# Adapters' products in float32r parts, and the values' bias joined to the output's, in a two-layer transformer kernel

## The chip, the cores and the metric

The kernel runs on one core of a Trainium2 chip. The core's engines work side by side, each through its own list of instructions in order, and wait for one another by semaphores: TensorE (PE, matrix products), VectorE (DVE), ScalarE (ACT), GpSimd (POOL) and SyncE (SP), which here issues most of the transfers (DMAs). SBUF is the memory on the core, with 128 partitions; a product's result lands in PSUM.

The metric is the device time of one execution in microseconds (us), the median of several runs. Before the change it is 2222.36 us, with runs from 2220.96 to 2223.24.

## The reference

Two layers over x of 8 batches x 512 tokens x 512 channels, all float32. Each has an attention and a feed-forward part, and a layer normalisation follows each part:

```python
x = layernorm(x + attention0(x))     # 16 heads of 32, causal, biases on Q, K, V and O
x = layernorm(x + experts(x))        # 8 experts, the best 2 of each token
x = layernorm(x + attention1(x))     # 8 query heads of 64, 2 key/value heads
x = layernorm(x + ffn(x))            # 1408 hidden, integer weights with scales
```

The change touches the first two. In attention0 the values and the output are

```python
v = x @ WV.T + WV_b
...
return softmax(scores) @ v @ WO.T + WO_b
```

and each expert has low-rank adapters (rank 16) on its two weights:

```python
gup = gup + 2.0 * (x @ gup_lora_A.T) @ gup_lora_B.T
...
out = out + 2.0 * (h @ down_lora_A.T) @ down_lora_B.T
```

## The kernel before

**Attention0** goes through the batches one by one. A batch has four groups g of four heads, and a group has three units u of key blocks: block 0, blocks 1 and 3, block 2. At each step (g, u), TensorE computes the scores (L1356), ScalarE the exponential (L1360), and GpSimd sets the part above the diagonal to zero (L1365, the mask); the product with the values (L1380) is issued one step later, so that TensorE has other work in between. This other work is listed by `plan` for each (g, u): products for values, queries (L1292) and keys (L1300) of the next group, the output projection, turning and routing of the batch before, and merges. A scheduler orders each engine's instructions by its own estimates when the program is built; for the first two products and from the second half of batch 7 to the end of the tail TensorE keeps the order as written. On the chip each engine runs its list in that fixed order. `normalise` sums the exponentials with a product (rs, L1395), then come a copy on ACT (r_inv, L995), a reciprocal on DVE (L1398, 3.34 us), the multiplication into aoT, and a guard's total on GpSimd (g_total, L998).

**Values** are copied out of PSUM by DVE, which adds the bias from `row`, a tile with both bias rows on all partitions (L1287). The output's bias, `row`'s second half, is added to x itself by GpSimd, one instruction of 128x2048 for each batch (L1474).

**The adapters** are merged into the experts' weights in SBUF before use: W + 2AB. One merge (L786) treats one of 6 blocks of 128x512 of two neighbouring experts: two products ps_lora of 16 rows (L781), then for each a copy with factor 2 on ACT (scaled, L792) and an addition to the weight on GpSimd (L794). There are 24 merges: six at (2,0) and six at (3,0) of batches 1 to 6, two after the last scores, and ten around the first tile steps of the experts. The factors lie in the tile `lora`, four experts at a time, at partitions 0, 32, 64 and 96 (16 rows each); its second load is issued in batch 7. Copies `scaled` share two buffers of 128x512 (tag r_inv) with r_inv.

**After attention0** comes a stretch that this text calls the tail: the steps of the first expert tiles (each step: products gate and up ps_gu, turning of h, product down ps_y), and between them the last batch's projection, turning, routing (ps_logits, choose, dispatch with ps_rank, one-hot tables with ps_table) and the merges. Then run the rest of the expert tiles, attention1 and the ffn, whose products take their left operand as a high and a low half in float32r (L1143).

Of the kernel before, what the change touches and what calls it, by code (L numbers as in the profile page):

```python
# [9 lines left out]
F32 = mybir.dt.float32  # L10
# [8 lines left out]
P = 128  # L19
NB = 8  # L20
S = 512
# [22 lines left out]

RARE = 3
LORA = 3 * 512 + 256
EXPERT = UPS * 512

SUM_LOW, SUM_HIGH = 1e-20, 1e20
# [1 line left out]
WIDEST = 2048.0  # L51


V_BQ, V_BK, V_NS, V_SS, V_SG, V_SU = 0, 4, 8, 12, 16, 16 + NHID
N_VEC = 16 + 2 * NHID


def in_order(tc, *engines):
# [46 lines left out]
class Env:  # L105
# [53 lines left out]
    def load_adapters(self, pool):  # L159
        nc, ins = self.nc, self.ins  # L160
        self.lora_sb = pool.tile([P, 2, LORA], F32, name="lora_sb")
        for i in range(2):
            for j in range(4):
                nc.sync.dma_start(out=self.lora_sb[32 * j : 32 * j + R, i, :], in_=ins.lora[i, j])
        self.wr = pool.tile([P, ND, E], F32, name="wr")
        nc.sync.dma_start(out=self.wr, in_=ins.w_router)
        self.ra = pool.tile([R, D], F32, name="ra")
        nc.sync.dma_start(out=self.ra, in_=ins.router_lora_a)
        self.rb = pool.tile([R, E], F32, name="rb")
        nc.sync.dma_start(out=self.rb, in_=ins.router_lora_b)  # L170
# [246 lines left out]
class Router:  # L417
# [4 lines left out]
    def __init__(self, env, keep, pool, small, tmp, dram):  # L422
        nc = env.nc
        self.env, self.nc, self.keep, self.small = env, nc, keep, small
        self.results = dram.tile([(N_FIXED + N_FREE) * P, D], F32, name="results")
        self.rows = dram.tile([NB * S, D], F32, name="rows")
        n = NB * NT
        self.hots = pool.tile([P, TOP_K, n, E], F32, name="r_hots")
        self.weights = keep.tile([P, TOP_K, n], F32, name="r_weights")

        self.ranks = pool.tile([P, TOP_K, n], F32, name="r_ranks")
        self.to_column = pool.tile([P, TOP_K, n], F32, name="r_to_column")
        self.table = pool.tile([P, E * E_TILES], F32, name="r_table")
        nc.gpsimd.memset(self.table, 0.0)
        self.carry = pool.tile([P, E], F32, name="r_carry")
        nc.vector.memset(self.carry, 0.0)


        self.wr = pool.tile([P, ND, 32], F32, name="r_wr")
        nc.vector.memset(self.wr, 0.0)  # L440
        self.gather = pool.tile([P, E], F32, name="r_gather")
        for c in range(ND):
            at = slice(32 * c, 32 * (c + 1))
            nc.vector.tensor_copy(self.gather[at, :], env.ident[at, 32 * c : 32 * c + E])
        scratch = tmp.tile([P, S], F32, tag="r_inv", name="r_scratch", bufs=2)
        self.ra = scratch[:R, :]
        self.rb = tmp.tile([R, E], F32, name="r_rb")

        def numbers(name, shape, pattern, base=0):
            i = tmp.tile([P, *shape], I32, name=f"{name}_i")  # L450
            nc.gpsimd.iota(i, pattern=pattern, base=base, channel_multiplier=0)
            f = pool.tile([P, *shape], F32, name=name)
            nc.vector.tensor_copy(f, i)
            return f


        self.iota = numbers("r_iota", [NT, E], [[0, NT], [1, E]], base=-E)
        self.part = numbers("r_part", [NT, E], [[0, NT], [E_TILES, E]])
        self.tiles = numbers("r_tiles", [N_FREE], [[1, N_FREE]])
        i = tmp.tile([P, 1], I32, name="r_lane_i")  # L460
        nc.gpsimd.iota(i, pattern=[[0, 1]], base=0, channel_multiplier=1)
        self.lane = pool.tile([P, 1], F32, name="r_lane")
        nc.vector.tensor_copy(self.lane, i)
        i = tmp.tile([P, S], F32, tag="r_inv", name="r_columns_i", bufs=2)[:, : E * E_TILES].bitcast(I32)
        nc.gpsimd.iota(i, pattern=[[1, E * E_TILES]], base=0, channel_multiplier=0)
        self.columns = pool.tile([P, E * E_TILES], BF16, name="r_columns")
        nc.vector.tensor_copy(self.columns, i)

        self.ones = pool.tile([P, P], F32, name="r_ones")
        nc.gpsimd.memset(self.ones, 1.0)  # L470
        self.before = pool.tile([P, P], F32, name="r_before")
        nc.gpsimd.affine_select(out=self.before, in_=self.ones, pattern=[[1, P]], compare_op=ALU.is_gt, fill=0.0,
                                base=0, channel_multiplier=-1)
# [277 lines left out]
class Experts:  # L751
# [17 lines left out]
                                   in_=src.rearrange("u p f -> p u f"))  # L769
            at += n * 512  # L770

    def load_lora(self, pool, i):

        self.lora = pool.tile([P, LORA], F32, tag="lora", name=f"lora_{i}")
        for j in range(4):
            self.nc.sync.dma_start(out=self.lora[32 * j : 32 * j + R, :], in_=self.env.ins.lora[i, j])

    def delta(self, ps, e, c):
        j = 32 * (e % 4)
        a, bt = lora_factors(self.lora[j : j + R, :], c)  # L780
        self.nc.tensor.matmul(ps, lhsT=a, rhs=bt, start=True, stop=True)  # L781

    def chunk(self, e, c, n=1):
# [13 lines left out]
class Tiles:  # L797
# [137 lines left out]
        self.hs[0], self.ats[0] = h, self.order[0][1] * EXPERT  # L935
        self.gate_up_to(0, ps("ps_gu"), lambda: None)

    def step(self):
        i = self.next
        self.next += 1  # L940
        if i + 1 < self.n:
            self.gate_up(i + 1, lambda: self.turn_hidden(i))
        else:
            self.turn_hidden(i)
        for n in range(4 if i == 0 else 5, 6):
            if i + n < self.BY_BLOCKS:
                self.fetch(i + n)
        if i + 10 >= self.BY_BLOCKS:
            self.fetch(i + 10)
        self.down(i)  # L950
        if i + 3 < self.BY_BLOCKS:
            self.turn_rows(i + 3)
        if i + 6 >= self.BY_BLOCKS:
            self.pair_back(i + 6)
        if i + 7 >= self.BY_BLOCKS:
            self.blocks(i + 7)
# [257 lines left out]
def attention0(env, guard, keep, routes, experts, dram, p_mm, tiles_ctx):  # L1214
# [8 lines left out]
    with ExitStack() as phase:  # L1223
# [30 lines left out]
        load_xT(0)  # L1254
        load_w(wk, 2, first)
        load_w(wv, 0)
        row = work.tile([P, 2, D], F32, name="row")
        nc.sync.dma_start(out=row, in_=ins.rows.partition_broadcast(P))
        load_w(wq, 1, others)
        load_w(wk, 2, others)  # L1260
        router = Router(env, keep, routes, small, work, dram)
# [3 lines left out]
        for i in range(N_FIXED + N_FREE - RARE, N_FIXED + N_FREE):  # L1265
            nc.sync.dma_start(out=router.results[ts(i, P), :], in_=guard.total)
        load_w(wo, 3)
        experts.load_lora(work, 0)
        for e in range(4):
            experts.load(e)  # L1270

# [7 lines left out]
        def mm(shape, name):  # L1279
            return p_mm.tile(shape, F32, tag="mm", name=name)  # L1280

        def value(b, t):
            ps = mm([P, D], "ps_v")
            for c in range(ND):
                nc.tensor.matmul(ps, lhsT=xts[b][:, c, ts(t, P)], rhs=wv[:, c, :], start=c == 0, stop=c == ND - 1)  # L1285
            vs[t] = own.tile([P, D], F32, tag=f"v{t}", name=f"v{t}")
            nc.vector.tensor_tensor(vs[t], ps, row[:, 0, :], ALU.add)  # L1287

        def query(b, g):
            ps = mm([P, S], "ps_q")  # L1290
# [119 lines left out]
        def plan(b):  # L1410
# [21 lines left out]
                    todo[3, 0].append(merge)  # L1432
            if b == 0:
                todo[1, 0].append(lambda: router.merge_lora(mm([P, ND, E], "ps_wr")))
            if b > 1:
                todo[0, 2].append(lambda: dispatch(b - 2))
                todo[1, 1].append(lambda: enter(one_hot(b - 2, range(NT))))
# [12 lines left out]
                tiles.fetch(i, room[:, i, :])  # L1450

        def begin():
            pair = work.tile([P, 2, D], F32, tag="row", name="first_turned")
            one = work.tile([P, S], F32, tag="logits", name="first_turned")
            tiles.begin([pair[:, 0, :], pair[:, 1, :], one], work.tile([P, 256], F32, name="first_h"),
                        lambda name: mm([P, S], name))

        def soon():
# [8 lines left out]
        for b in range(NB):  # L1467
            todo = plan(b)
            for g in range(ND):
                if g == 2:  # L1470
                    if b + 1 < NB:
                        load_xT(b + 1)

                    nc.gpsimd.tensor_tensor(xs[b], xs[b], row[:, 1:2, :].to_broadcast([P, NT, D]), ALU.add)  # L1474
                if g == 3 and b + 1 < NB:
                    load_x(b + 1)
                if b == NB - 1 and g == 1:
                    experts.load_lora(work, 1)
                    experts.load(4)
                if b == NB - 1 and g == 2:  # L1480
                    order.enter_context(in_order(tc))
# [32 lines left out]
            merge()  # L1514
        for c in range(ND):
            turn(b, c)
        tiles.step()
        score(b)
        merge()
# [3 lines left out]
        dispatch(b)  # L1523
        for places in ((0, 1), (2, 3)):
            rows = one_hot(b, places)
            tiles.step()
            merge()
        enter(rows)
        tiles.of_fixed = router.fixed(routes)
        while merges:  # L1530
            tiles.step()
            merge()
        order.close()
    return router, tiles, router.tables(routes, p_mm.tile([P, E], F32, tag="mm", name="ps_count"), guard.routed[:, 1:2])
# [569 lines left out]
def _layout(a):  # L2104
# [26 lines left out]
    def columns(n):  # L2131
        return a[n].transpose(0, 2, 1).reshape(2, 4, R, -1)

    lora = np.concatenate([rows("L0_ffn_gup_lora_A"), columns("L0_ffn_gup_lora_B"), columns("L0_ffn_down_lora_B"),
                           rows("L0_ffn_down_lora_A")], axis=3)
    return {
        "x": x,
        "xT": x.transpose(0, 2, 1),
        "w_attn0": np.concatenate([(by_group if n in "QK" else units)(a[f"L0_attn_W{n}_w"].T) for n in "VQKO"]),
        "vecs": np.concatenate(  # L2140
            [cols(a[n]) for n in ("L0_attn_WQ_b", "L0_attn_WK_b", "L1_attn_norm_scale", "L1_attn_split_scale",
                                  "L1_ffn_s_gate", "L1_ffn_s_up")], axis=1),
        "rows": np.stack([a["L0_attn_WV_b"], a["L0_attn_WO_b"]]),
        "w_router": a["L0_ffn_gate_weight"].T.reshape(ND, P, E).transpose(1, 0, 2),
        "router_lora_a": a["L0_ffn_gate_lora_A"],
# [26 lines left out]
```

## Time and profile before

One execution was profiled. It took 2228.55 us, of which the core's span from first to last instruction is 2226.8; it ran 6.2 us above the median of the three timed runs.

| stage (us of the span) | length | PE busy | DVE | ACT | POOL | granted clock |
|---|---|---|---|---|---|---|
| batch 0 of attention0 (0 to 90) | 90 | 84.52 | 36.88 | 27.65 | 27.89 | 1.00 |
| batches 1 to 7 (90 to 720) | 630 | 621.75 | 397.00 | 188.75 | 191.16 | 1.00 |
| end of attention0, tail (720 to 830) | 110 | 105.03 | 61.83 | 31.87 | 38.26 | 0.91 |
| expert tiles (830 to 1185) | 355 | 353.24 | 111.74 | 81.77 | 82.31 | 1.00 |
| attention1 (1185 to 1700) | 515 | 514.32 | 402.37 | 167.48 | 127.12 | 1.00 |
| ffn (1700 to 2226.8) | 526.8 | 512.98 | 263.88 | 134.45 | 20.88 | 0.99 |

The table is from the view by windows: the busy time of each engine in a stretch, and the mean clock that the throttle granted TensorE (1.00 is full speed). A busy TensorE is one with products in flight; it need not be at its peak. In a timeline's lines stand the start in us, the time up to the end of a group of like instructions, engine, line of the code, operation, output and inputs with their shapes, and in brackets the idle time of the engine ahead of it and the engine whose work ended it. A row of the waits names an engine's instruction, whom it waited for, the total in us, how often, and the longest.

In the page's list of groups, the 96 records of the adapters' products (L781, two for each product) have 36.7 us busy, the 48 copies L792 27.1 (599 ns each), the 48 additions L794 62.0 (1313 ns), and the 8 additions of the bias to x L1474 37.2 (4650 ns).

### The profile page before, as it was taken

The numbers are of one execution on the slowest core, as the hardware profiler recorded it, in microseconds if no ns is written. First come the engines' busy times: TensorE is split into PE (matmuls) and PEld (weight loads), VectorE is DVE, ScalarE is ACT, GpSimd is POOL, SyncE is SP. The second block draws the span as 40 slices with busy tenths as digits, with TensorE's granted clock in tenths as the row PEclk, the third lists the DMA queues.
The fourth block names the chain that finished last, engine by engine and source line by source line (L and its number), as shares of the span: only waits on it lengthen the run. The fifth ranks groups of instructions, "written<-read, shape, count | busy, mean of one in ns | idle before, by whom it ended". The sixth has DMA issues, their size and how long they took to land. (4 is left out here: it accounts for less than half of the span.)

```text
span 2226.8 us, 23678 instructions
## 1 busy us (share of the span) xinstructions
PE 2191.9 (98%) x9006; PEld 1116.6 (50%) x9006; DVE 1273.7 (57%) x2032; ACT 632.0 (28%) x917; POOL 487.6 (22%) x489
## 2 busy tenths in 40 slices
PE   9999999999999999999999999999999999999997
PEld 3344444444444444444443333333343778888876
DVE  3556666666666633323316887798757655555443
ACT  2332323323233232122124333223332222222222
POOL 2322423234132333122105222222211000000000
PEclk9999999999999899999999999999999999999999
DMA  8010101101022216888735212312110321111000
GB/s 297 20 57 1 57 10 48 58 1 58 5 71 94 85 57 181 227 218 214 191 114 193 80 57 86 95 55 77 45 32 13 109 78 57 57 57 57 20 20 21
DMA packets 146428, 182.20 MB, mean 82 GB/s; under 512 B 60530, under 2 KB 89202, under 8 KB 144514
## 3 DMA queue, kind: packets, MB, share of 16 engines
q1 hardware_dynamic: 135024, 144.91, 21.0%
q0 software_dynamic: 10560, 34.61, 5.5%
q8 instruction: 74, 1.21, 0.2%
q10 hardware_dynamic: 722, 1.07, 0.1%
q14 instruction: 48, 0.39, 0.1%
HBM read 117.38 MB, written 63.18 MB: 81 GB/s over the span
## 5 line engine op out<-in xcount | busy, mean ns | idle before, releaser
L903 PE MATMUL ps_gu<-experts,xrT 128*128 128x512 f32 (+1 forms) x520 | 248.8, 601 | 0.0
L1360 ACT ACTIVATE p<-sc 128x2048 f32<-128x2048 f32 (+1 forms) x96 | 152.8, 1592 | 190.0 <-PE sc L1356 183.1
L1148 DVE SCALAR_TENSOR_TENSOR hT<-ps_u,vec,sg 128x512 f32<-128x512 f32 x88 | 65.6, 745 | 195.2 <-PE ps_u L1143 195.2
L1365 POOL TENSOR_SCALAR_AFFINE_SELECT p<-p 128x512 f32<-128x512 f32 x128 | 91.6, 729 | 385.2 <-ACT p L1360 378.5
L1159 PE MATMUL ps_f<-ffn_w,h_half 128*128 128x512 f32 x672 | 170.2, 394 | 0.6 <-issue 0.4
L998 POOL TENSOR_TENSOR g_total<-g_total,r_inv 128x512 f32<-128x512 f32 x64 | 89.7, 1401 | 358.3 <-DVE r_inv L1735 283.0
L1705 ACT ACTIVATE p<-sc 128x1024 f32<-128x1024 f32 x128 | 124.0, 1021 | 105.9 <-PE sc L1702 100.8
L1735 DVE RECIPROCAL r_inv<-r_inv 128x512 f32<-128x512 f32 x32 | 107.1, 3346 | 78.8 <-ACT r_inv L995 78.8
L1388 DVE TENSOR_TENSOR p<-p 128x1536 f32<-128x1536 f32 (+2 forms) x96 | 129.4, 1348 | 39.2 <-POOL p L1365 22.2
L905 DVE TENSOR_TENSOR h<-ps_gu,h 128x256 f32<-128x256 f32 x67 | 28.4, 424 | 212.8 <-ACT h L904 212.8
L903 PEld LDWEIGHTS ps_gu<-experts,xrT 128*128 128x128 f32 x520 | 96.2, 197 | 89.7 <-issue 89.5
L1159 PEld LDWEIGHTS ps_f<-ffn_w,h_half 128*128 128x128 f32 x672 | 124.4, 188 | 33.0 <-DVE h_half L1154 5.6
L1143 PE MATMUL ps_g<-x_high,ffn_w 128*128 128x512 f32 x352 | 138.9, 395 | 0.8 <-DVE x L1676 0.8
L1143 PE MATMUL ps_g<-x_low,ffn_w 128*128 128x512 f32 x352 | 139.1, 395 | 0.0
L1143 PE MATMUL ps_u<-x_low,ffn_w 128*128 128x512 f32 x352 | 138.8, 394 | 0.0
L1143 PE MATMUL ps_u<-x_high,ffn_w 128*128 128x512 f32 x352 | 138.7, 394 | 0.0
L919 PE MATMUL ps_y<-experts,hT 128*128 128x512 f32 (+1 forms) x272 | 127.9, 593 | 0.5 <-ACT hT L913 0.5
L1702 PE MATMUL sc<-qT,kT 64*128 64x512 f32 x512 | 127.3, 615 | 1.0 <-ACT qT L1609 0.7
L1292 PE MATMUL ps_q<-experts 128*128 128x512 f32 x256 | 121.1, 615 | 4.4 <-DMA experts<-in_xT 4.4
L1724 PE MATMUL av<-p,v 128*64 128x512 f32 x512 | 123.8, 605 | 0.0
L1285 PE MATMUL ps_v<-experts 128*128 128x512 f32 x256 | 118.0, 609 | 3.3 <-DVE v L1287 3.3
L1670 PE MATMUL ps_o<-attn_out,aoT 128*128 128x512 f32 x256 | 117.9, 605 | 0.8 <-ACT r_inv L995 0.8
(262 smaller groups left out, 3438.5 us busy)
## 6 DMA issues: line engine op xcount, KB each, us to landing
results<-y SPq DMA_DIRECT2D x68, 256.0 KB, 2.3
turned<-turned SPq DMA_DIRECT2D x56, 256.0 KB, 4.1
pair<-xrT SPq DMA_DIRECT2D x25, 512.0 KB, 3.4
xrT<-pair SPq DMA_DIRECT2D x100, 128.0 KB, 4.5
x<-in_x SPq DMA_DIRECT2D x8, 1024.0 KB, 7.5
experts<-in_gate_up SPq DMA_DIRECT2D x8, 1024.0 KB, 10.8
rows<-x SPq DMA_DIRECT2D x32, 256.0 KB, 2.0
x<-rows SPq DMA_DIRECT2D x8, 1024.0 KB, 15.5
```

The costliest lines, as they stand in the source:

```text
L903: nc.tensor.matmul(ps, lhsT=xT[:, c, :], rhs=self.weights(i, c), start=c == 0, stop=c == ND - 1)
L919: self.nc.tensor.matmul(ps, lhsT=hT[:, c, :], rhs=self.weights(i, ND + c), start=c == 0, stop=c == self.NI - 1)
L1143: nc.tensor.matmul(ps, lhsT=w[:, ts(dc, P)], rhs=x[:, dc, :], start=(dc, i) == (0, 0), stop=(dc, i) == (ND - 1, 1))
L1159: self.nc.tensor.matmul(os[t], lhsT=h[:, ts(t, P)], rhs=self.weights(2 * NHID + c), start=(c, i) == (0, 0), stop=(c, i) == (NHID - 1, 1))
L1285: nc.tensor.matmul(ps, lhsT=xts[b][:, c, ts(t, P)], rhs=wv[:, c, :], start=c == 0, stop=c == ND - 1)
L1292: nc.tensor.matmul(ps, lhsT=wq[:, g, ts(c, P)], rhs=xts[b][:, c, :], start=c == 0, stop=c == ND - 1)
L1360: nc.scalar.activation(p, sc[:, :, :width], AF.Exp, scale=scale)
L1388: nc.vector.tensor_tensor(total[:, :, P * kt :], total[:, :, P * kt :], p[:, :, at : at + w], ALU.add)
L1670: nc.tensor.matmul(ps, lhsT=state[b]["aoT"][:, c, ts(t, P)], rhs=w_out[:, c, :], start=c == 0, stop=c == ND - 1)
L1702: nc.tensor.matmul(sc[:, j, :], lhsT=st["kT"][hs, ts(kt, P)], rhs=st["qT"][g][hs, :], start=True, stop=True)
L1705: nc.scalar.activation(p, sc, AF.Exp, scale=scale)
L1724: nc.tensor.matmul(st["av"][HD * j : HD * (j + 1), :], lhsT=st["v"][:, kt, HD * j : HD * (j + 1)], rhs=p[:, j, :], start=kt == 0, stop=kt ...
```

## The change

**Adapters.** The factors are no longer multiplied as float32. Each is split into a high part (its value rounded to float32r) and a low part (the rest), and the four products of parts are computed as one product: the 16 rows of a factor are repeated four times in the input, so that an expert has 64 rows and a pair of experts all 128 partitions. In rows 0 to 15 of an expert stand high parts of both factors, in the others high and low, low and high, low and low. `masks` makes two columns of signs and of zeros and ones from the bits of the partition's number; with them `split_part` makes the parts: ACT copies the raw values with the sign as factor and rounds (l_high), GpSimd multiplies the raw values by 0 or 1 and adds l_high, so that a row has either the high part or raw minus high. A pair's 1792 columns are fetched and split in four pieces (512, 512, 512, 256). There is one buffer for the raw piece; the next piece's fetch is issued after the split of the one before. l_high shares the two r_inv buffers.

The pieces are split in batch 0 at (2,1), (2,2), (3,1), (3,2), in batches 4 and 7 at (0,0), (0,2), (1,0), (1,2), and the last pair's in the tail, two around each of two tile steps, where merges stood. The last six merges now go two a tile step, one in the middle of it and one behind it, over three steps.

**Bias of the values.** Rows of softmax sum to one, so the bias of v passes through to WV_b @ WO.T. `join_bias`, once in batch 0 at (1,2), computes this with four products and adds it to `row`, which now has only the output's half. The copies of the values are plain ones, by DVE for the even and ACT for the odd blocks (`evacuate`). The addition of `row` to x[0] now comes after join_bias.

The two rooms that the first tiles took from `row` are now one from it and one from the raw piece's buffer. The path for rare inputs is adapted (it does not run here), and the input layouts follow. The diff, cut:

```diff
...
-V_BQ, V_BK, V_NS, V_SS, V_SG, V_SU = 0, 4, 8, 12, 16, 16 + NHID
-N_VEC = 16 + 2 * NHID
+V_BQ, V_BK, V_NS, V_SS, V_SG, V_SU, V_BV = 0, 4, 8, 12, 16, 16 + NHID, 16 + 2 * NHID
+N_VEC = V_BV + 4
+LORA_PARTS = 4
...
-    def load_lora(self, pool, i):
-        self.lora = pool.tile([P, LORA], F32, tag="lora", name=f"lora_{i}")
-        for j in range(4):
-            self.nc.sync.dma_start(out=self.lora[32 * j : 32 * j + R, :], in_=self.env.ins.lora[i, j])
+    def masks(self, pool, lane):
+        nc = self.nc
+        bits = pool.tile([P, 2], I32, name="l_bits")
+        self.low = pool.tile([P, 2], F32, name="l_low")
+        self.sign = pool.tile([P, 2], F32, name="l_sign")
+        for i, bit in enumerate((2 * R, R)):
+            nc.vector.tensor_scalar(bits[:, i : i + 1], lane, bit, None, ALU.bitwise_and)
+        nc.vector.tensor_copy(self.low, bits)
+        nc.vector.tensor_scalar(self.low, self.low, 1.0, None, ALU.min)
+        nc.vector.tensor_scalar(self.sign, self.low, -2.0, 1.0, ALU.mult, ALU.add)
+        self.parts = [(q, c) for q in range(E // 2) for c in range(LORA_PARTS)]
+
+    def fetch_part(self, pool):
+        if self.parts:
+            q, c = self.parts[0]
+            at, n = 512 * c, min(512, LORA - 512 * c)
+            self.raw = pool.tile([P, 512], F32, tag="raw", name="l_raw")
+            self.nc.sync.dma_start(out=self.raw[:, :n], in_=self.env.ins.lora[q, :, at : at + n])
+
+    def split_part(self, pool):
+        nc = self.nc
+        q, c = self.parts.pop(0)
+        if c == 0:
+            self.lora = pool.tile([P, LORA], F32R, tag="lora", name=f"lora_{q}")
+        at, n = 512 * c, min(512, LORA - 512 * c)
+        i = int(c in (1, 2))
+        high = pool.tile([P, 512], F32R, tag="r_inv", name="l_high", bufs=2)[:, :n]
+        nc.scalar.activation(high, self.raw[:, :n], AF.Copy, scale=self.sign[:, i : i + 1])
+        raw = self.raw[:, :n]
+        nc.gpsimd.tensor_scalar(raw, raw, self.low[:, i : i + 1], None, ALU.mult)
+        nc.gpsimd.tensor_tensor(self.lora[:, at : at + n], raw, high.bitcast(F32), ALU.add)
+        if (q, c) != (E // 2 - 2, LORA_PARTS - 1):
+            self.fetch_part(pool)
 
     def delta(self, ps, e, c):
-        j = 32 * (e % 4)
-        a, bt = lora_factors(self.lora[j : j + R, :], c)
+        j = P // 2 * (e % 2)
+        a, bt = lora_factors(self.lora[j : j + P // 2, :], c)
         self.nc.tensor.matmul(ps, lhsT=a, rhs=bt, start=True, stop=True)
...
-    def step(self):
+    def step(self, amid=lambda: None):
...
             self.fetch(i + 10)
+        amid()
         self.down(i)
...
-        row = work.tile([P, 2, D], F32, name="row")
-        nc.sync.dma_start(out=row, in_=ins.rows.partition_broadcast(P))
+        row = work.tile([P, D], F32, name="row")
+        nc.sync.dma_start(out=row, in_=ins.rows[1].partition_broadcast(P))
...
-        experts.load_lora(work, 0)
+        experts.masks(work, router.lane_i)
+        experts.fetch_part(work)
         for e in range(4):
             experts.load(e)
...
-            nc.vector.tensor_tensor(vs[t], ps, row[:, 0, :], ALU.add)
+            env.evacuate(t, vs[t], ps)
+
+        def join_bias():
+            bv = work.tile([P, ND, P], F32, tag="r_inv", name="bv", bufs=2)
+            nc.vector.tensor_copy(bv, vec[:, V_BV : V_BV + ND, None].to_broadcast([P, ND, P]))
+            ps = mm([P, D], "ps_bias")
+            for c in range(ND):
+                nc.tensor.matmul(ps, lhsT=bv[:, c, :], rhs=wo[:, c, :], start=c == 0, stop=c == ND - 1)
+            nc.vector.tensor_tensor(row, ps, row, ALU.add)
...
+            if b == 0:
+                todo[1, 2].append(join_bias)
+            early = (0, 0), (0, 2), (1, 0), (1, 2)
+            slots = {0: ((2, 1), (2, 2), (3, 1), (3, 2)), 4: early, 7: early}
+            for slot in slots.get(b, ()):
+                todo[slot].append(lambda: experts.split_part(work))
...
-                    nc.gpsimd.tensor_tensor(xs[b], xs[b], row[:, 1:2, :].to_broadcast([P, NT, D]), ALU.add)
+                    nc.gpsimd.tensor_tensor(xs[b], xs[b], row[:, None, :].to_broadcast([P, NT, D]), ALU.add)
...
                 if b == NB - 1 and g == 1:
-                    experts.load_lora(work, 1)
                     experts.load(4)
...
         for c in range(ND):
             turn(b, c)
+        experts.fetch_part(work)
         tiles.step()
...
         for places in ((0, 1), (2, 3)):
             rows = one_hot(b, places)
+            experts.split_part(work)
             tiles.step()
-            merge()
+            experts.split_part(work)
         enter(rows)
         tiles.of_fixed = router.fixed(routes)
         while merges:
-            tiles.step()
+            tiles.step(merge)
             merge()
...
+    lora = np.repeat(lora.reshape(E // 2, 2, 1, R, LORA), 4, axis=2).reshape(E // 2, P, LORA)
```

## The prediction

> **What bounds the kernel now.** First the busy shares.
>
> ```profile
> PE 2191.9 (98%) x9006; PEld 1116.6 (50%) x9006; DVE 1273.7 (57%) x2032; ACT 632.0 (28%) x917; POOL 487.6 (22%) x489
> ```
>
> TensorE sets the time nearly everywhere: a change gains what it takes off PE and loses what it makes PE wait. PE's waits come next.
>
> ```profile
> PE sc L1356 <- ACT p L1360: 5.2, 7, 1.8
> ...
> PE av L1380 <- POOL p L1365: 0.3, 1, 0.3
> ```
>
> PE waits seven times for an exponential (5.2 us in all; one wait is 1.77, so the other six are 0.58 each) and once, in batch 0, for GpSimd's mask. The timeline shows where a merge stands.
>
> ```profile
> 232.46 1.03 PE L781 MATMUL ps_lora<-lora 16*128 16x512 f32 x4
> 233.41 0.64 PE L1380 MATMUL av<-p,v 128*32 128x256 f32 x8
> 234.63 1.15 PE L1356 MATMUL sc<-q,k 32*128 32x384 f32 x16 [0.58 <-ACT p L1360]
> ```
>
> ```profile
> 811.77 1.13 PE L781 MATMUL ps_lora<-lora 16*128 16x512 f32 x4
> 812.83 1.98 PE L903 MATMUL ps_gu<-experts,xrT 128*128 128x512 f32 x4
> ```
>
> A merge holds PE for 233.41 − 232.46 = 0.95 us in attention, where a wait follows at once, and for 812.83 − 811.77 = 1.06 in the tail, where none does. What one pass at float32r costs, layer 1's FFN shows: starts 0.24 apart.
>
> ```profile
> 1822.73 0.39 PE L1143 MATMUL ps_g<-x_high,ffn_w 128*128 128x512 f32 x1
> 1822.97 0.40 PE L1143 MATMUL ps_g<-x_low,ffn_w 128*128 128x512 f32 x1
> ```
>
> Last, batch 0, where four of the new splits and the bias go.
>
> ```profile
> 54.67 1.59 POOL L998 TENSOR_TENSOR g_total<-g_total,r_inv 128x512 f32<-128x512 f32 x1 [2.03 <-DVE r_inv L1398]
> 56.23 5.51 POOL L1474 TENSOR_TENSOR x<-x,row 128x2048 f32<-128x2048 f32 x1
> ...
> 61.68 1.81 POOL L1365 TENSOR_SCALAR_AFFINE_SELECT p<-p 128x512 f32<-128x512 f32 x3
> 62.37 1.07 PE L1380 MATMUL av<-p,v 128*32 128x512 f32 x8 [0.35 <-POOL p L1365]
> ...
> 68.61 0.69 ACT L1302 ACTIVATE k<-ps_k,vec 128x512 f32<-128x512 f32 x1 [2.58 <-PE ps_k L1300]
> 69.50 1.14 PE L1356 MATMUL sc<-q,k 32*128 32x512 f32 x8
> ```
>
> One addition of 5.51 us on GpSimd holds up the mask behind it, and PE runs out of cover: GpSimd is 22% busy over the span but the limit here.
>
> **The gain: 24 merges.** A merge has two products of two passes each; starts of passes lie 0.43 apart, and the two products run side by side on different rows, 0.9 to 1.06 a merge. In float32r a product is one pass; if the pair still runs side by side, 0.24 to 0.4 is left, a gain of 0.63. Where it arrives differs:
> - Six merges at (2,0) of batches 1 to 6: the exponential sets the pace behind them, so the wait grows from 0.58 to 1.2 and nothing is gained.
> - Six at (3,0): the second product sits among the scores (253.94), and scores and merge take 253.93 to 255.86 = 1.93 against 235.71 − 234.63 = 1.08 for scores alone. Gain (1.93 − 1.08) − 0.2 = 0.65 each, 3.9.
> - Two after the last scores hold PE 737.63 to 742.64, 5.0 us, as a chain: product, ACT's copy (0.60 each), next product. Four copies and the first product stay, about 3.1: gain 1.9.
> - Ten in the expert tiles: 10 × 0.63 = 6.3.
> - The 0.74 that PE waits for ACT's copy ahead of the table (820.70) goes, since no merge stands there now: 0.7.
> Sum −12.8. The bounds: nothing where a longer wait swallows all (the six at (3,0) and the ten: −2.6), or 24 × 0.7 + 2.6 = −19.4 where none does.
>
> The Trainium skill, "TensorEngine Tiling (Array Packing)", in Key Properties, says that a change of tiling mode makes the array drain; a 64-row product amid 32-row scores would be one. The 16-row products among the scores showed no gap (253.94, 253.95). By the page, at an estimate of 0.3 a time from the length of a 32-row score pass (8 of them in 1.14 us, two of those), six such places would take 1.8 off the gain, and the sum would be +11.6; no run here shows it.
>
> **Values.** Their evacuation is still one pass from PSUM (0.69 on DVE before; now two on DVE, two on ACT at 0.60 to 0.69). PE's four waits for them (3.3 us in all) come from DVE's chain for the routing, and v0 remains on DVE behind it: 0, bounds −3.3 to +1.
>
> **The bias, on PE's path.** join_bias adds four float32 products 128x512 in batch 0's (1,2): 8 records × 0.43 = 3.44. They wait for a copy on DVE (0.68) that stands behind a reciprocal (51.25 to 54.6), while PE is ready at 54.4: 0.9. Sum +4.4; bounds +3.4 and +5.5.
>
> **Batch 0's splits.** Each of 16 splits is: ACT copy 0.6, GpSimd multiplication by a value per partition (nearest row L721: 1.56 alone, 2.54 beside gathers; I take 1.65), GpSimd addition (L722 1.26 to 1.59, L794 mean 1.31; 1.35), then the next fetch, of 256 KB (rows of that size land in 2.0 to 2.3, the 112 KB of the old adapter loads in 3.0 to 4.3; 3.1). There is one buffer, so the next ACT copy stands in ACT's order until its fetch lands, and all later work of ACT with it.
> - First stall. The first copy needs the buffer of g_total's operand, free at 56.3: copy 57.0, multiplication 58.7, addition 60.1. In the order built for GpSimd, both row additions of x follow (the one of 19.69, which now needs the joined row, and the one of 56.23), at 4.5 to 5.5 each: 69.3; then the mask, 69.95. PE wants it at 62.0 + 4.4 = 66.4: +3.5. Before, 5.5 us of addition were just covered (0.35); that cover is spent.
> - Second stall. ACT's order has r_inv, copy 1, p(2,2), copy 2, k(3). From r_inv at 72.2: 0.6 + 1.65 + 1.35 + 3.1 + 0.6, then k's 0.69, gives 80.2, or 80.9 with the mask and g_total of GpSimd between; PE is ready at 69.5 + 4.4 + 3.5 = 77.4: +3.5.
> - After each wait PE runs slower, below: +3.2.
> Sum +10.2; bounds 0 (fetch and splits in half the time) and +14.
>
> **The clock.** A wait of 1.77 us at 722.9 is followed by
>
> ```profile
> 720.00:724.00 4.00, 2.23 (x26) 0.86 (x22) 3.33 (x19) 2.00 (x2) 0.66 (x1) 0.91 0.67 258
> 724.00:728.00 4.00, 4.00 (x28) 1.96 (x24) 3.41 (x20) 1.88 (x1) 1.22 (x2) 0.50 0.02 4
> 728.00:732.00 4.00, 3.41 (x24) 1.38 (x16) 3.99 (x10) 2.17 (x5) 0.39 (x1) 0.74 0.00 0
> ```
>
> the eighth column being the granted clock: 0.50 for 3.4 to 6 us, so 1.7 to 3 us of work lost. One of 1.71 at 277.3 does the same; the waits of 0.58 do not. The six waits of 1.2 us lie between: 0 to 6 × 1.7 = +10 by that; I take one loss, +2. The skill's "TensorE: Matmul & The Clock Gate", Part 1: The HAM clock gate, wants a whole idle window of some 3.4 us; the row at 724 contradicts it with 1.77. By the page this term would be 0 and the sum +7.8.
>
> **Batches 4 and 7.** A split's copy stands before k(1) of ACT, at 0.3 to 1.2 each: +1. SP's order gets three small fetches between the loads of experts 4 and 5 (660.3 and later), whose first use is in the tail, tens of us on: 0, and at most a fetch's 3 us each if that slack were gone. In batch 0 one fetch replaces four of 112 KB ahead of the experts' loads: 0. The masks are five instructions on single columns at the start, the third room of begin only a new place: 0.
>
> **The tail.** Four splits fall around three tile steps, each fetch starting after the addition. ACT's copies stand ahead of h and hT: h 0.7 late; the next hT waits for a chain of 2.5 us of older additions and three times (GpSimd 3.0, fetch 2.8, copy 0.6), 21.2 after the ranks, where PE is there at 19.0, so 2.6 to 3.4 with hT's own copy; then the last six merges, two a step, need 2 × 1.3 on GpSimd each, and the gathers for later tiles (0.95) queue behind: 1.5. Sum +5; bounds 0 and +9.
>
> **Sum.** −12.8 + 4.4 + 10.2 + 2 + 1 + 5 = +9.8. The profiled execution took 2228.55 us (span 2226.8), so 2238.4 in its terms. It lay 6.2 above the median of the runs, 2222.4, which I carry over: 2232.2.
>
> **Rivals.**
> - *Everything hides* (faster). GpSimd and ACT have slack, the fetches land in 2 us, nothing waits in batch 0 or the tail. For it: 22% and 28% busy. Against it: the 0.35 at 62.37, where one addition already overran. Then −12.8 + 4.4 = −8.4: 2214.0. It decides if a split takes under 3 us from copy to landed fetch.
> - *Half of it hides* (no change). Only batch 0's first stall and its clock appear, 3.5 + 1.5, and 3.5 in the tail: −12.8 + 4.4 + 8.5 = +0.1, 2222.5.
> - *The clock falls at every (2,0)* (slower still). Six waits of 1.2 us each bring half speed: +8 more, and the tail costs 9: 2232.2 + 8 + 4 = 2244.
> - *The pair doesn't run side by side*. 64-row products in turn cost 0.46 a merge, 16 × 0.23 = 3.7 less gain: 2236; within the forecast's range.
>
> **How the numbers follow.** Forecast with its fourth rival 0.48 (own range 2226 to 2239), everything hides 0.22, half hides 0.18, clock at every (2,0) 0.12. The measurement can tell 0.2%, 4.4 us. Forecast and last case lie above 2226.8, half hides between the bounds, everything hides below 2217.9: slower 0.60, same 0.18, faster 0.22. The range leaves out half of "everything hides" below 2213 and most of the last case above 2243.
>
> **What would show it.** Right: in batch 0 an av waiting for GpSimd's p for some 3.5 us and a sc for ACT's k for another 3.5, clock 0.50 behind each; four ps_bias products of 3.4 us; ps_lora in two records that take 0.25 to 0.4 together; (2,0) waits of 1.2 without half clock; an hT or ps_y in the tail waiting for ACT 2 to 3 us. Wrong: no wait over 1 us in 55 to 85 (first rival), clock 0.5 after each (2,0) (third), or ps_lora records 0.43 apart (no gain at all: 2245). What would upset it most: a fetch much faster than 3 us.

## The result, and the profile after

The change makes the kernel slower, by 0.3%: 2229.61 us (median of 12 runs, 2227.26 to 2233.28) against 2223.34 (12 runs, 2220.96 to 2226.88); ratio 1.0026, 95% interval 1.0018 to 1.0034. The forecast was 2232, slower.

Busy shares after, from the page's first part:

```profile
PE 2177.5 (98%) x8966; PEld 1111.3 (50%) x8966; DVE 1270.7 (57%) x2023; ACT 650.1 (29%) x949; POOL 528.5 (24%) x521
```

TensorE is busy for 14.4 us less than in the first profile of before (2191.9), and 6.7 less than in a second one (2184.2, with the experiments); most of what these two differ by is clock, 23.9 and 10.2 us at half speed ahead of the last instructions. Yet the time rose: more of it is spent waiting. The waits of TensorE after (waiter, whom it waited for, total us, times, longest):

```profile
PE av L1426 <- POOL p L1411: 4.1, 1, 4.1
...
PE ps_y L954 <- ACT hT L948: 3.3, 2, 2.8
PE sc L1402 <- ACT k L1348: 3.0, 2, 2.2
```

The three hardly stood in the profile of before (0.3, 0.5 and 0.8). The waits for the exponential, at the head of that view, grew from 5.2 to 7.8: six of 0.58 are 1.0 now. Of the three, the wait for the mask and most of that for k are in batch 0. TensorE there, from the timeline:

```profile
70.53 1.07 PE L1426 MATMUL av<-p,v 128*32 128x512 f32 x8 [4.07 <-POOL p L1411]
71.42 1.86 PE L1441 MATMUL rs<-p,ones 128*32 128x512 f32 x8
...
81.94 1.14 PE L1402 MATMUL sc<-q,k 32*128 32x512 f32 x8 [2.21 <-ACT k L1348]
```

and the two engines that it waits for, GpSimd and then ScalarE:

```profile
60.90 8.99 POOL L1525 TENSOR_TENSOR x<-x,row 128x2048 f32<-128x2048 f32 x2
69.83 1.83 POOL L1411 TENSOR_SCALAR_AFFINE_SELECT p<-p 128x512 f32<-128x512 f32 x3
```

```profile
80.60 0.72 ACT L805 ACTIVATE l_high<-l_raw,l_sign 128x512 fp32r<-128x512 f32 x1 [4.98 <-DMA l_raw<-in_lora]
81.22 0.67 ACT L1348 ACTIVATE k<-ps_k,vec 128x512 f32<-128x512 f32 x1
```

The mask that TensorE wants at 66.5 stands behind one split (57.11 to 60.9) and both additions of `row` (8.99 together), and comes at 69.83. The copy of k stands behind a copy of raw factors whose fetch has not landed. The rs behind the first wait take 1.86 instead of 1.04; the windows give the reason (the eighth column is the granted clock):

```profile
66.00:70.00 4.00, 0.46 (x2) 0.00 (x0) 0.75 (x1) 0.54 (x1) 4.00 (x2) 1.00 0.00 0
70.00:74.00 4.00, 3.47 (x24) 0.93 (x24) 1.76 (x1) 0.60 (x3) 1.65 (x3) 0.69 0.00 0
```

After TensorE's 4.07 us of nothing, the clock is down once, for 3.4 us at half speed (0.69 here and 0.89 in the next four: the missing 0.31 and 0.11 of 4 us each make 1.7 us, the half of 3.4); from 78 on, around the second wait, it is 1.00. Such a stretch of 3.4 us is called a half-clock window below.

Where the merges stand, TensorE after, at (2,0):

```profile
244.54 0.49 PE L816 MATMUL ps_lora<-lora 64*128 64x512 f32 x2
244.97 0.64 PE L1426 MATMUL av<-p,v 128*32 128x256 f32 x8
```

A pair side by side holds TensorE 0.43, in the tail as well (848.07 to 848.50), where it was 0.95 to 1.06. At (3,0), before (batch 2) and after (batch 1):

```profile
252.31 1.12 PE L781 MATMUL ps_lora<-lora 16*128 16x512 f32 x2
253.36 0.64 PE L1380 MATMUL av<-p,v 128*32 128x256 f32 x8
253.93 0.58 PE L1356 MATMUL sc<-q,k 32*128 32x384 f32 x1
253.94 0.69 PE L781 MATMUL ps_lora<-lora 16*128 16x512 f32 x1
253.95 0.92 PE L1356 MATMUL sc<-q,k 32*128 32x384 f32 x5
...
255.86 1.13 PE L1292 MATMUL ps_q<-experts 128*128 128x512 f32 x2
```

```profile
171.25 0.49 PE L816 MATMUL ps_lora<-lora 64*128 64x512 f32 x1
171.68 0.64 PE L1426 MATMUL av<-p,v 128*32 128x256 f32 x8
172.32 0.91 PE L1402 MATMUL sc<-q,k 32*128 32x384 f32 x2
173.16 0.50 PE L816 MATMUL ps_lora<-lora 64*128 64x512 f32 x1
173.59 1.14 PE L1402 MATMUL sc<-q,k 32*128 32x384 f32 x14
174.66 0.70 PE L1338 MATMUL ps_q<-experts 128*128 128x512 f32 x1
```

Here a merge's two products stand apart, the first ahead of the products with the values, the second among the scores. The first held TensorE 1.05 (two passes) and holds 0.43. The second ran beside the scores before (253.93 to 253.95); now one score's two passes run alone, then the product alone, then the other scores, and the stretch from the first score to ps_q takes 2.34 instead of 1.93.

The kernel of before was profiled a second time with the experiments (span 2219.4, time 2221.15, nearer the median than the first). Like products of the two programs were laid side by side, and the difference of their starts followed through the span:

| stretch | start after − start before, at its end | step | forecast |
|---|---|---|---|
| first transfers | 1.1 | +1.1 | 0 |
| join_bias | 5.3 | +4.2 | +4.4 |
| two waits in batch 0 and the clock | 13.3 | +8.0 | +10.2 |
| batches 1 to 7, merges at (2,0) and (3,0) | 14.7 | +1.4 | −3.9 + 1 + 2 |
| merges and tail, up to the tables | 6.0 | −8.7 | −8.9, late merges included |
| last pair's splits, late merges | 11.1 | +5.1 | +5 |
| attention1 and ffn | 7.9 | −3.2 | 0 |

The two profiled executions differ by 8.1 (2227.5 − 2219.4), the medians by 6.3. The 1.1 of the first transfers belongs to the execution: the run below with the first splits in batch 1 starts as after does and lacks it. The +1.4 of batches 1 to 7 is −0.8 at (3,0), +1.3 in waits for values (3.3 against 2.0) and +0.9 in the clock at the end of batch 7; the last two differ from one execution to the next.

### The profile page after: what moved, and what is told of

The parts are those of the page before. It is cut to its first block, busy times and chain, and to the rows that moved or that the text cites. A ratio compares the mean times of both kernels' runs of the same rounds, so it can differ in the third digit from the quotient of the medians.

```text
span 2227.5 us, 23696 instructions
## 1 busy us (share of the span) xinstructions
PE 2177.5 (98%) x8966; PEld 1111.3 (50%) x8966; DVE 1270.7 (57%) x2023; ACT 650.1 (29%) x949; POOL 528.5 (24%) x521
## 5 line engine op out<-in xcount | busy, mean ns | idle before, releaser
L1340 DVE TENSOR_SCALAR q<-ps_q,vec 128x512 f32<-128x512 f32 x32 | 24.0, 751 | 180.4 <-PE ps_q L1338 180.4
```

## The experiments

All times are medians but for the last; each ratio is to runs of the kernel before on the same chip. "Fastest" is "both remedies, bias as before".

| kernel | us | ratio, 95% interval |
|---|---|---|
| after | 2229.61 | 1.0026 (1.0018 to 1.0034) |
| before, again | 2223.24 | 0.9998 (0.9989 to 1.0007) |
| bias alone | 2228.90 | 1.0022 (1.0011 to 1.0032) |
| after, first splits in batch 1 | 2223.46 | 0.9999 (0.9988 to 1.0009) |
| after, last pair fetched at once | 2226.28 | 1.0014 (1.0003 to 1.0025) |
| both remedies | 2219.33 | 0.9976 (0.9967 to 0.9985) |
| both remedies, bias as before | 2214.10 | 0.9955 (0.9942 to 0.9967) |
| splits in batch 0, bias as before | 2220.43 | 0.9984 (0.9974 to 0.9993) |
| before, vec wider | 2222.11 | 0.9991 (0.9983 to 1.0000) |
| fastest, buffers at 64 | 2217.26 | 0.9979 (0.9967 to 0.9991) |
| fastest, buffers at 96 | 2216.57 | 0.9966 (0.9955 to 0.9978) |
| both remedies, products over 128 rows | 2218.49, one run | |

**Before, unchanged.** No edit.

> The kernel of before, unchanged, profiled a second time. Its median should be 2223 again. The two profiled executions differ in layer 1's FFN: starts of products there are 0.2327 us apart on average before and 0.2312 after, some 3.4 us over the FFN, though no part of the change touches it. If that belongs to the one execution that was profiled, this profile shows another average; if it belongs to the program (its place in memory), it shows 0.2327 again and the change would gain 3.4 us there that nobody meant.

Two products of the FFN in this profile, and the same two in the profile after:

```profile
1735.01 0.39 PE L1159 MATMUL ps_f<-ffn_w,h_half 128*128 128x512 f32 x1
...
2185.76 0.39 PE L1143 MATMUL ps_u<-x_high,ffn_w 128*128 128x512 f32 x1
```

```profile
1745.93 0.62 PE L1195 MATMUL ps_f<-ffn_w,h_half 128*128 128x512 f32 x2
...
2193.77 0.39 PE L1179 MATMUL ps_u<-x_high,ffn_w 128*128 128x512 f32 x1
```

450.75 us lie between them before and 447.84 after, over 1936 starts: 0.2328 us each and 0.2313 (the expectations count 0.0001 less). The first profile of before has 0.2328 as well. So the FFN's gain of some 3 us belongs to the program and not to the execution, though the change does not touch the FFN.

**Before, with the buffers moved.**

```diff
-N_VEC = 16 + 2 * NHID
+N_VEC = 16 + 2 * NHID + 4
```

> Before, with nothing changed but vec four columns wider (38 to 42), which moves every later buffer by 16 bytes. If the FFN's shorter spacing (0.2312 instead of 0.2327 on average) comes from where its buffers lie, the spacing is 0.2312 here too and the time 2223.4 - 3.3 = 2220. Rival, it comes from another part of the bias change: 0.2327 and 2223.4.

In the built program the later buffers lie 32 bytes further on, not 16, since rooms are rounded up. Spacing 0.2313, as after; by the same two products the FFN gains 2.9 us. The time is 2222.11; against the runs of before on its chip (2224.64) that is −2.5, with an interval that reaches 1.0000, so it is the spacing that shows it. The two later runs below, with the buffers 64 and 96 bytes from where before has them, show 0.2337 and 0.2332. So the FFN's gain comes from where the buffers lie, and not by a rule of 64 bytes.

**The bias alone.**

```diff
-            nc.vector.tensor_tensor(vs[t], ps, row[:, 0, :], ALU.add)
+            env.evacuate(t, vs[t], ps)
...
+            if b == 0:
+                todo[1, 2].append(join_bias)
```

> Before, with only the bias joined to the output's and the plain copies of the values; adapters as before. Theory: the four products cost 4.2, and since the addition of the row to x[0] now follows them on GpSimd, both additions (4.5 each) stand ahead of the masks of batch 0's third group: row ready at 59.6, masks at 69.3 where PE is there at 66.5, a wait of 2.5 to 3 where it was 0.35, perhaps with one half-clock window (1.7): 2223.3 + 4.2 + 2.5 + 0.9 = 2231. Rival 1, only the products count: 2227.5. Rival 2, the plain copies of the values give back what the products cost: 2223.

Measured 2228.90, and 2231 less the FFN's 3 is 2228. TensorE waits 2.88 for the mask without a single split in the program. GpSimd of this kernel:

```profile
59.61 8.98 POOL L1484 TENSOR_TENSOR x<-x,row 128x2048 f32<-128x2048 f32 x2 [3.46 <-DVE row L1296]
68.55 1.80 POOL L1374 TENSOR_SCALAR_AFFINE_SELECT p<-p 128x512 f32<-128x512 f32 x3
```

Both additions start when the joined row is there (59.61) and hold up the masks for 9 us. Before, the first of them ran at 19.69, long before anything needed GpSimd. The bias part alone loses 5.4 us against before on its chip, nearly as much as the whole change. In the trace, by the starts of like products, its products cost 4.2 and the wait behind the addition that had to move 2.5, and the FFN gives 3.2 back. Another 4.8 come in batches 2 to 6 of this execution, with longer waits for values (5.3 in all, against 2.0 in the second profile of before) and a half-clock window behind one of them; whether the plain copies have a part in that is not shown.

**First pair's splits in batch 1.**

```diff
-            slots = {0: ((2, 1), (2, 2), (3, 1), (3, 2)), 4: early, 7: early}
+            slots = {1: early, 4: early, 7: early}
```

> After, with the first pair's four splits in batch 1 at the early steps that batches 4 and 7 use, none in batch 0. Theory: the wait of sc for k (2.21) goes, of the wait of av for GpSimd's mask (4.07) only the 1.2 that the split stood ahead of the additions goes, since the two additions make the rest, and batch 1 has no new wait over 1 us: 2229.6 - 2.2 - 1.2 - 0.8 = 2225.5. Rival 1, the splits make both waits: 2229.6 - 6.3 - 1.7 = 2221.6. Rival 2, the splits cost the same wherever they stand: 2229.6.

Measured 2223.46, 6 us less than after. The wait for k is gone, the wait for the mask (68.08) still 2.89, as the theory had it. In the trace, the difference to after is −1.3 (first transfers) at the start, −5.1 at the end of batch 0 and −6.2 in batch 5; at the head of batch 2 there is one new wait for values, of 0.97. That the time came out 2 below the theory's 2225.5 is of the size of that first difference and of the waits for values, which differ between executions.

**Last pair's factors fetched at once.**

```diff
+    def fetch_last(self, pool):
+        room = pool.tile([P, ND, 512], F32, tag="aoT", name="l_last")
+        self.nc.sync.dma_start(out=room.rearrange("p c s -> p (c s)")[:, :LORA], in_=self.env.ins.lora[E // 2 - 1])
+        self.last = [room[:, c, :] for c in range(LORA_PARTS)]
...
         experts.load(7)
+        experts.fetch_last(work)
...
-        experts.fetch_part(work)
```

> After, with the last pair's raw factors fetched in one transfer, ahead of the tail's tile steps, into the buffer that aoT leaves free, so that no split in the tail waits for a fetch; the work of ACT and GpSimd on them is the same. Theory: the chain of fetches set the tail's waits; ps_y's wait for hT (2.76), ps_hT's for h (0.59) and the half-clock window behind them (1.7) go: 2229.6 - 5 = 2224.6. Rival: GpSimd's chain of splits, additions and gathers sets the tail, and the wait only moves to the merges behind: 2228 to 2229.6.

Measured 2226.28, between the two. After, TensorE and ScalarE in the tail:

```profile
825.66 0.50 PE L816 MATMUL ps_lora<-lora 64*128 64x512 f32 x2
828.92 3.48 PE L954 MATMUL ps_y<-experts,hT 128*128 128x512 f32 x4 [2.76 <-ACT hT L948]
```

```profile
828.10 0.51 ACT L805 ACTIVATE l_high<-l_raw,l_sign 128x256 fp32r<-128x256 f32 x1 [5.04 <-DMA l_raw<-in_lora]
828.52 0.35 ACT L948 COPY hT<-ps_hT 128x256 f32<-128x256 f32 x1
```

and with the single fetch:

```profile
816.48 0.44 PE L953 MATMUL ps_hT<-ident,h 128*128 128x128 f32 x2 [1.47 <-DVE h L947]
```

The wait of 2.76 and the half-clock window behind it are gone, and a wait of 1.47 stands in their place (by the starts of like products the tail gains 4.7, by the medians 3.3): now ScalarE's copies wait for GpSimd's 2.9 us a split (the last until 815.14), and h (815.55) stands behind them. Both theories were half right.

**Both remedies, and with the bias as before.** The second is the first with the value's bias on DVE, both halves of `row`, and the raw pieces in the buffer of the logits, since there is no room for one of their own beside a whole `row`; a pair's first piece is then fetched in the last step of the batch before its splits.

```diff
-            env.evacuate(t, vs[t], ps)
+            nc.vector.tensor_tensor(vs[t], ps, row[:, 0, :], ALU.add)
...
-                todo[1, 2].append(join_bias)
...
-            self.raw = pool.tile([P, 512], F32, tag="raw", name="l_raw")
+            self.raw = pool.tile([P, 512], F32, tag="logits", name="l_raw")
```

> After, with both remedies for the splits (first pair's in batch 1, last pair's factors fetched at once into aoT's buffer) and the joined bias kept. If the two remedies add up: 2229.6 - 6.1 - 3.3 = 2220.2. Against the kernel without the joined bias it tells what the bias costs in batch 0: theory 4.2 of products and 2.5 of wait of av for GpSimd's mask, so 6.7 and perhaps half a clock window more than that kernel.

> The adapters' parts alone, with their splits where they cost least: the values' bias is added by DVE as before and row keeps both halves (no join_bias), the first pair's splits stand in batch 1, the last pair's raw factors are fetched at once into aoT's buffer, and the other raw pieces take the buffer of the logits (there is no room for one of their own). Theory: from the 2223.5 of the splits in batch 1, less 3.3 (the tail, as measured) and less the bias's products and the addition behind them (4.2 + 2.5): 2213.5, faster than before by 10. Rival: in the bias kernels layer 1's FFN gains 3.3 us that come with the bias; without it they are lost and the time is 2217. If the FFN's gain comes from vec's four more columns, which this kernel keeps, it stays.

2219.33 and 2214.10: the remedies add up, and the second kernel is the fastest of all, 0.45% below before. Some 3 of these 10.5 us are the FFN's, from the four columns of vec, which this kernel keeps and does not use. At the end of batch 0 the one with the joined bias is 7.1 us later by the trace, beside the 0.6 of the first transfers (4.2 products, 3.0 the wait), but only 5.2 by the median. In the two profiled executions, 2.4 more are lost at the end of batch 7, where the clock falls in the one with the joined bias alone, and 3.9 come back at 740, where the fastest kernel shows a wait that the other lacks:

```profile
PE ps_lora L823 <- DVE first_h L947: 3.4, 1, 3.4
```

The reason is in the clock (eighth column) and in DVE's timeline. This kernel's:

```profile
724.00:728.00 4.00, 3.53 (x33) 1.52 (x32) 3.88 (x19) 2.53 (x5) 1.50 (x3) 1.00 0.03 6
```

```profile
734.99 1.37 DVE L581 TENSOR_SCALAR one_hot<-r_columns,r_to_column 128x256 bf16<-128x256 bf16 x1
```

and those of its twin with buffers at 64, with the same order of instructions:

```profile
724.00:728.00 4.00, 4.00 (x24) 0.91 (x16) 3.93 (x17) 0.84 (x3) 1.22 (x2) 0.50 0.01 2
```

```profile
734.44 0.28 DVE L581 TENSOR_SCALAR one_hot<-r_columns,r_to_column 128x256 bf16<-128x256 bf16 x1
```

In the first the clock stays up behind the wait of 1.76, and TensorE's merge starts at 733.74. GpSimd adds two merged blocks at 735.01 to 737.51, the two instructions of DVE beside them take 1.3 instead of 0.3, and first_h, behind them on DVE, comes at 738.42. In the second the clock falls, the merge starts at 735.51 and the additions at 736.78, behind first_h (735.80). Of the thirteen profiles two have the clock up there, this one and the next run's, and these two alone have the wait of 3.4: what the kernel is spared by the clock it loses again here.

**Splits in batch 0, bias as before.** The kernel just shown, with the slots of the change and the first fetch at (0,0) of batch 0.

> Bias added by DVE as before, with the first pair's splits left in batch 0, as the change has them (raw pieces in the logits' buffer, last pair's factors fetched at once). In GpSimd's order both additions to x now stand ahead of the first split. Theory: against the kernel with the joined bias and the same tail (2226.3) the products (4.2) and the wait of av for the mask (4.07) go, the wait of sc for k (2.2) behind the fetch stays: about 2217.5. Rival: the split alone holds up the masks as much as the two additions did, and the wait of av stays at 3 to 4: 2222.

Measured 2220.43, again between: the products are gone, TensorE waits 1.50 for a mask (58.07) and 2.33 for k (73.97). Here the first split alone holds up the mask, and its multiplication takes 3.10 (52.98). So the wait for k belongs to the fetch and the order of ScalarE, whatever the bias does. Of after's 4.07 the split makes 1.2, by the run with the splits in batch 1. This profile too has the wait of 3.4 for first_h.

**Products over 128 rows.** The kernel with both remedies, each product over all rows. It sums over both experts of the pair, so its merged weights are not those of the reference; it serves to price the product.

```diff
-        a, bt = lora_factors(self.lora[j : j + P // 2, :], c)
+        a, bt = lora_factors(self.lora, c)
```

> The kernel before this one in the list, but with each adapters' product taken over all 128 rows (it sums over both experts of the pair, so the merged weights are others), so that no product uses part of the array's rows. After, a pair of 64-row products holds TensorE 0.43 in the tail and in attention, and a single one at (3,0) also 0.43, where a float32r pass of 128 rows in the FFN takes 0.23. If the change between 64 and 128 rows costs the 0.2 (and 0.1 ahead of it), two 128-row products take 0.46 together in the tail and a single one at (3,0) 0.23. If a lone float32r product behind float32 ones costs 0.43 whatever its rows, the pair takes 0.86.

One run, 2218.49. Products at (2,0):

```profile
145.82 0.74 PE L823 MATMUL ps_lora<-lora 128*128 128x512 f32 x2
146.49 0.64 PE L1433 MATMUL av<-p,v 128*32 128x256 f32 x8
```

Two take 0.67 (0.34 and 0.33). One alone at (3,0) takes 0.42 (165.57 to 165.99), as one of 64 rows does, so a second one adds 0.25. The second expectation is right for a lone product and wrong for the pair: the 0.2 extra comes once for the float32r products that stand together among the attention's, and not from 64 rows. The scores around the second product at (3,0) take 2.34 here too (166.64 to 168.98). In the tail, from the start of the turning ahead of the merge to the gate product behind it, two products of 128 rows in turn take 0.90 (823.53 to 824.43), and after's pair of 64 rows 0.96 (847.54 to 848.50). Side by side or in turn, a merge there costs nearly the same.

**Buffers at 64 and at 96 bytes.** Unused columns of vec added to the fastest kernel.

```diff
-N_VEC = V_BV + 4
+N_VEC = V_BV + 4 + 8
```

(16 in place of 8 for the second.)

> The fastest kernel so far (e5_best, 2214.1) with vec widened by eight more unused columns, which moves the FFN's buffers by 32 bytes more, to 64 from where before has them. If what counts there is the place modulo 64, products start 0.2327 apart again, as in before, and the time rises by 3.3 to 2217.4. If it isn't, the spacing tells another number.

> The same with sixteen more columns, buffers 96 bytes from where before has them. If the place modulo 64 counts: 0.2312 apart and 2214.1, as e5_best.

2217.26 and 2216.57, spacings 0.2337 and 0.2332: the first as expected in time, but the second shows that the place modulo 64 is not the rule.

## Why the prediction was right

- **The bias** was forecast at +4.4 for its products and measured at 4.2. That its row holds up the addition to x[0], and this the masks, was the first stall's working; the run with the bias alone shows it as the main part (2.88, against after's 4.07).
- **The first stall**, +3.5, measured 3.7 more than before. **The second stall**, +3.5, measured 2.2: the fetch landed after 2.8 (forecast 3.1) and the multiplication took 1.57 (1.65).
- **The clock.** After the first wait one window of 3.4 us at half clock, after the second none: batch 0's waits and clock came to 8.0 instead of 10.2. (The rows at 720 to 732 were read as 3.4 to 6 us at half clock; their missing 0.09, 0.50 and 0.26 of 4 us each make 6.8.) The six waits of 1.0 at (2,0) brought no window, where one was taken (+2). Ahead of the last instructions half clock takes 17.1 us after and 10.2 and 23.9 in the two profiles of before, so no gain or loss of it is settled at that size. The granted clock fell behind the wait of 1.76 at the end of batch 7 in eleven of the thirteen profiles, behind the wait of 2.9 for the mask in one of the four that have it, and behind that of 4.07 in both that have it. The Trainium skill, "TensorE: Matmul & The Clock Gate", Part 1: The HAM clock gate, has a window that runs free of the kernel, which agrees with the first two counts; that it needs a whole idle window, the 1.76 contradicts.
- **Merges at (2,0)**, gain 0: right, the wait for the exponential took it (0.58 to 1.0).
- **Merges at (3,0)**, gain 0.65 each, 3.9: wrong. By the starts of like products it is 0.13 to 0.14 each, 0.8. The step that failed is "(1.93 − 1.08) − 0.2": it looked for the gain in the stretch of the scores and took the second product there at 0.2. That stretch grew, from 1.93 to 2.34. In each of the six merges the first product, which the forecast left out, gains 0.63, and the second, with what waits around it, loses 0.50. Part of the loss may be a wait, since the trace puts 0.55 ahead of the product's weight load down to ScalarE's copy of the logits; what keeps the scores from running beside it is not shown. The 0.3 a place that the prediction left out of its sum, as a drain, points the right way; no run tells whether a drain is the reason.
- **Batches 4 and 7**, +1 for copies of splits ahead of k: not seen. TensorE's waits for k outside batch 0 are 0.8 before and after.
- **Merges in the tail, after the last scores and ahead of the table, and the last pair's splits**: −8.9 + 5 = −3.9 forecast, −8.7 + 5.1 = −3.6 measured, with the wait where it was said, of TensorE for hT (2.76).
- **Values**, forecast 0 with bounds −3.3 to +1: TensorE waits for them 3.3 us before, 3.3 after, 2.0 in the second profile of before and 5.3 with the bias alone. They differ by 1.3 between two executions of one program, so an effect of the change at that size is not settled.
- **What was not in the sum:** the FFN's 3.2 us by the place of its buffers. By luck it cancels the 3.1 that are missing at (3,0). The sum came out near (2232.2 against 2229.6) with two terms wrong by 3 each, of opposite sign; the 2.6 that are left have the size of batch 0's 2.2, since smaller differences cancel. That the change loses, and mostly in batch 0, was no luck: the two waits, the bias's products and the tail came where they were forecast.

The rival "everything hides" is refuted by its place, 66 to 82 us; nothing hid until splits, fetches and bias were moved away. That kernel's 2214.1 is near the rival's 2214.0 by chance: it has no bias products, which the rival counts at 4.4, and has the FFN's 3.2, which the rival does not count. "Half of it hides" (2222.5) fell with the second wait in batch 0. "Clock at every (2,0)" did not happen in any run. "The pair doesn't run side by side" holds at (3,0) alone.

## What to carry to other kernels

Work taken off the bounding engine is paid back where its preparation enters another engine's order: find what stands behind each new instruction on ScalarE and GpSimd, and put it where that engine has several microseconds to spare, with its data fetched well before. A constant that is folded into another one makes everything that reads the other wait for the folding; look where the reader was placed before. Measure with the old program profiled twice before a gain or loss of 0.2% is given to an edit.

## What the runs showed of the hardware

- The spacing of the FFN's float32r products depends on where their buffers lie: 0.2328 us on average as in before (two profiles), 0.2312 to 0.2313 with the buffers 32 bytes further (nine kernels), 0.2337 at 64 and 0.2332 at 96. Over 1936 products the ends lie 4.8 us apart, more than most edits of this study. What decides it is open.
- A lone float32r product of 512 columns between products of 32 columns or rows holds TensorE 0.42 to 0.43, with 64 rows or 128; a second one behind it adds 0.25. In the FFN one takes 0.23.
- DVE's bf16 comparisons for the one-hot tables take 0.24 to 0.30 alone and 1.3 when a GpSimd addition runs. The skill's "SBUF — State Buffer", Who interferes with whom, names an exclusive lock between these two engines; the 1.3 beside GpSimd's 1.25 an addition agrees. Beside GpSimd's multiplication of a split they took 0.24 to 0.63 (from 812.17 and from 815.08, with the last pair fetched at once), so a lock like that is not seen there.
- A GpSimd multiplication by a value per partition over 128x512 took 1.56 when nothing ran on DVE (81.42, after) and 1.57 inside a reciprocal of DVE (74.86), but 2.48 to 3.10 beside DVE's additions to p (57.11, after; 52.98 with the splits in batch 0 and the bias as before).
